# Wo multiplied into the experts' first layers and gates while edges are scattered; first layers stopped at the last node

## The chip, the core and the metric

The kernel runs on one core of one Trainium2 chip. The metric is device time in microseconds from start to end of one execution. The core's engines run side by side, each with its own instructions in a fixed order: PE (matrix multiplication, results in the PSUM memory), DVE (vectors), ACT (scalar functions and copies), POOL (here mostly for scattering by index) and SP (here a queue that starts DMA transfers). An instruction starts when its engine is free and the semaphores it waits for have been raised. Working data lie in the on-chip SBUF memory; DRAM holds inputs, outputs and scratch tensors.

## The reference

Two layers of a graph network work on 1250 nodes of 512 channels and 40000 edges. Layer 0 adds edge attention and a global linear attention to the nodes, and then a block with causal attention and a mixture of eight experts. Layer 1 has a graph convolution, an additive attention and a memory of products of keys. The change concerns the causal block and one feed-forward layer ahead of it:

```
hx = _layernorm(x, ln_g, ln_b)
q, k, v = hx @ Wq, hx @ Wk, hx @ Wv
...
attn = softmax(where(causal, q @ k.T, lowest))
o = attn @ v
y = o.transpose(0, 2, 1, 3).reshape(b, n, d) @ Wo
gate = softmax(y @ gate_W + gate_b)
hid = gelu(einsum('bnd,edf->bnef', y, W1) + b1)
eo = einsum('bnef,efd->bned', hid, W2) + b2
out = einsum('bned,bne->bnd', eo, gate)
```

So y is used in two products only, with gate_W (512 x 8) and with each expert's W1 (512 x 256). The layer ahead is `h = silu(z @ W1.T + b1); ff = h @ W2.T + b2`, with 1024 hidden channels.

## The kernel before

All data are float32, except one-hot matrices in bfloat16. The nodes are padded from 1250 to 1280 (NP) and lie in NT = 10 tiles of P = 128; the last tile has TAIL = 98 real ones. Activations that a matmul sums over lie transposed, channels on partitions, as [128, KC = 4, 1280]. Matmuls over all nodes go by three chunks of columns (CHUNKS): 512, 512 and 256. A float32 matmul stands in the profile as two records, a transpose as one.

The stages follow each other in the program:

1. **Edges.** POOL scatters 40000 edge weights into a table in DRAM (adj, 1280 x 1280 x 9 numbers) with 313 indirect DMAs (line 341). DVE compares keys (lines 315 and 325), PE counts with the one-hot matrices (line 307). `pump` lets the edges advance a few batches whenever a piece of other work has been written down, so that layer 0's linear attention and the projections of the edge attention stand among them. This stage has no order written by hand: a scheduler sets the order of instructions on each engine. Its last part is the pool gqkv (lines 521 to 575): keys and queries (kT, q_d), values (line 548), then two products of weights for layer 1. The first is gcn_Wg times dense_W, kept in DRAM as wgd_d (lines 556 to 562); then come a row of biases (bsum_d, line 568) and fold_q (lines 569 to 574, on PE as tr<-bd). Weights here share the tag "w" with three buffers, outgoing blocks the tag "qs" with three. DMAs of this part are issued on SP.
2. **Edge attention** (lines 581 to 737): for each tile a slab of adj (5760 KB) and its queries are loaded on SP (load_tile, lines 588 to 596). The first slab waits for the scatters and for everything that lay in its place in SBUF. Scores are line 617, ACT's copy of the counts is line 601, DVE's mask line 609.
3. **Feed-forward** (lines 787 to 875): the edge attention's output, then first_layer (lines 804 to 810), 8 blocks of channels by three chunks, and the second layer by tiles (line 857). On its way it loads the four weights of the causal block (fw, line 847).
4. **Causal attention** (lines 884 to 1131), with an order written by hand on PE, DVE and ACT: a loop over 40 steps (tile t, pair of heads m). A step's PE work is, in this order: transposes of one head's weights (turn, e = 0, line 1034), the preparation of a coming tile (turn_heads as ut, hx, heads, projected), turn for e = 1, divide and output for a tile that is done, the next scores (sc), and values (av, line 1047). In the step in which output stands, hx and turn_heads stand too, as long as a tile is left to prepare. ACT and DVE keep the same order: ACT does turn's copies, two exponentials (line 1023), the copies fkT and qt (line 980) and two quarters of h (line 930); DVE does the maxima (line 1007), the other two quarters of h (line 933), and the copies of turn for e = 1 (wT, line 1036), which av reads. DVE's h waits for ACT's h. output (lines 1070 to 1075) multiplies a tile's attention by Wo, 16 matmuls of 128 columns (y), and DVE copies the result into yT.
5. **Experts** (lines 1140 to 1474): gate_logits multiplies yT by gw (gate_W padded to 32 columns), hidden multiplies yT by an expert's W1 (chan_mm, in all three chunks), expert_out by its W2. load_expert fetches the next but one expert's weights on SP.
6. **Layer 1** (lines 1475 to 1841).

Nearly all plain matmuls go through `mm`, so their line is 177; their tiles' names tell them apart.

Of the kernel before, what the change touches and what calls it, by code (L numbers as in the profile page):

```python
# [11 lines left out]
F32 = mybir.dt.float32  # L12
# [55 lines left out]
def tile_gps_layers(ctx: ExitStack, tc: tile.TileContext, a, out):  # L68
# [40 lines left out]

    fold_q = const.tile([P, KC, HG], F32, name="fold_q")  # L110
    nc.gpsimd.memset(fold_q, 0.0)
    cols = const.tile([P, NCOL], F32, name="cols")
    nc.scalar.dma_start(cols, a["cols"])

# [61 lines left out]
        for i, (l, r) in enumerate(pairs):  # L176
            nc.tensor.matmul(ps, lhsT=l, rhs=r, start=i == 0, stop=i == len(pairs) - 1)  # L177

    def node_mm(ps, xT, t, w, n0=0, n1=C):

        mm(ps, [(xT[:, c, t * P:(t + 1) * P], w[:, c, n0:n1]) for c in range(xT.shape[1])])

    def chan_mm(ps, w, m, xT, c0, cn):

# [8 lines left out]
    xb_d = dram.tile([NP, C], F32, name="xb_d")  # L193
    att_d = dram.tile([P, KC, NP], F32, name="att_d")
    deg_d = dram.tile([P, NP], F32, name="deg_d")
    wgd_d = dram.tile([P, KC, C], F32, name="wgd_d")
    bsum_d = dram.tile([P, C], F32, name="bsum_d")

# [322 lines left out]
    with tc.tile_pool(name="gqkv", bufs=2) as pq:  # L521
        gbv = rows_bc(pq, a["gnn_rows"][0:2], 2, name="gbv")
        wk = load_w(pq, "gnn_WkT", KC, C, bufs=3)
        wq = load_w(pq, "gnn_WqT", KC, C, bufs=3)
        wv = load_w(pq, "gnn_WvT", KC, C, bufs=3)
        zT = pq.tile([P, KC, NP], F32, name="zT", bufs=1)
        for t in range(NT):
            z = pq.tile([P, C], F32, tag="z", name="z")
            norm(pq, z, xn[:, t, :], 1e-5, "lnz")
            transposed(zT, z, t, "att_g", "att_b")  # L530
            xb = pq.tile([P, C], F32, tag="xb", name="xb")
            nc.vector.tensor_tensor(xb, xn[:, t, :], gbv[:, 1, :], op=OP.add)
            nc.scalar.dma_start(xb_d[t * P:(t + 1) * P, :], xb)
        for c0, cn in CHUNKS:
            for m in range(KC):
                ps = ps_mm()
                chan_mm(ps[:, :cn], wk, m, zT, c0, cn)
                nc.vector.tensor_scalar(kT[:, m, c0:c0 + cn], ps[:, :cn], col("gnn_bk", m), None, op0=OP.add)
                ps = ps_mm()
                chan_mm(ps[:, :cn], wq, m, zT, c0, cn)  # L540
                qs = pq.tile([P, 512], F32, tag="qs", name="qs", bufs=3)
                nc.scalar.activation(qs[:, :cn], ps[:, :cn], AF.Identity, bias=col("gnn_bq", m))
                nc.sync.dma_start(q_d[:, m, c0:c0 + cn], qs[:, :cn])
                pump(1)
        for t in range(NT):
            ps = ps_mm()
            node_mm(ps, zT, t, wv)
            nc.vector.tensor_tensor(va[:, t, :], ps, gbv[:, 0, :], op=OP.add)
            pump(1)


        brow = rows_bc(pq, a["l1_rows"], len(L1_ROWS), name="l1rows")
        wg = load_w(pq, "gcn_WgT", KC, C, bufs=3)
        wd = load_w(pq, "L1_gnn_W_dense", KC, C, bufs=3)
        wqn = load_w(pq, "l1_Wq", KC, C, bufs=3)
        for m in range(KC):
            ps = ps_mm()
            mm(ps, [(wg[:, c, m * P:(m + 1) * P], wd[:, c, :]) for c in range(KC)])
            qs = pq.tile([P, 512], F32, tag="qs", name="qs", bufs=3)
            nc.scalar.copy(qs, ps)  # L560
            nc.sync.dma_start(wgd_d[:, m, :], qs)
            pump(1)
        ps = ps_mm()
        mm(ps, [(col("gcn_b", c).to_broadcast([P, P]), wd[:, c, :]) for c in range(KC)])
        qs = pq.tile([P, 512], F32, tag="qs", name="qs", bufs=3)
        nc.vector.tensor_tensor(qs, ps, brow[:, 0, :], op=OP.add)
        nc.vector.tensor_tensor(qs, qs, brow[:, 1, :], op=OP.add)
        nc.sync.dma_start(bsum_d, qs)
        bd = pq.tile([P, KC, H], F32, name="bd")
        nc.vector.tensor_tensor(bd, own_head, col("l1_wq", 0, 4)[:, :, None].to_broadcast([P, KC, H]), op=OP.mult)  # L570
        ps = ps_tr((P, KC, H))
        for m in range(KC):
            mm(ps[:, m, :], [(wqn[:, c, m * P:(m + 1) * P], bd[:, c, :]) for c in range(KC)])
        nc.scalar.copy(fold_q[:, :, :H], ps)
        pump(EC)
    s_edge.close()
    s_xn.close()
# [167 lines left out]

    X = ctx.enter_context(tc.tile_pool(name="X", bufs=1)).tile([P, NT, C], F32, name="X")
    s_y = ctx.enter_context(ExitStack())
    yT = s_y.enter_context(tc.tile_pool(name="fy", bufs=1)).tile([P, KC, NP], F32, name="yT")
    s_fw = s_y.enter_context(ExitStack())
    pfw = s_fw.enter_context(tc.tile_pool(name="fw", bufs=1, side="right"))  # L750

# [35 lines left out]
    with tc.tile_pool(name="gff", bufs=1) as pf, tc.tile_pool(name="gffw", bufs=2) as pw:  # L787
# [16 lines left out]
        def first_layer(c, m):  # L804
            c0, cn = CHUNKS[c]
            if m == 0:
                hTs[c] = pw.tile([P, 8, 512], F32, tag="hT", name="hT")
            ps = ps_mm()
            chan_mm(ps[:, :cn], w1, m, zT, c0, cn)
            nc.scalar.activation(hTs[c][:, m, :cn], ps[:, :cn], AF.Silu, bias=col("gnn_b1", m))  # L810
# [5 lines left out]
        with tc.manual_schedule(engines={nc.tensor.engine, nc.vector.engine, nc.scalar.engine}):  # L816
            for t in range(NT + 2):
# [26 lines left out]
                if t >= NT - 2:  # L844
                    for m in range(2 * (t - NT + 2), 2 * (t - NT + 3)):
                        first_layer(0, m)
            fw = [load_w(pfw, f"L0_ffn_W{x}", KC, C, tag="fw" + x) for x in "kqvo"]
            fetch_xm(0)
            fetch_xm(1)
            for c, (c0, cn) in enumerate(CHUNKS):  # L850
                n = cn // P
                for k, t in enumerate(range(c0 // P, c0 // P + n)):
# [1 line left out]
                        for m in range(8 * k // n, 8 * (k + 1) // n):  # L854
                            first_layer(c + 1, m)
                    ps = ps_mm()
                    node_mm(ps, hTs[c], k, w2)
                    nc.vector.tensor_tensor(X[:, t, :], ps, X[:, t, :], op=OP.add)
                    nc.vector.tensor_tensor(X[:, t, :], X[:, t, :], inputs.pop(t), op=OP.add)
                    if t + 2 < NT:  # L860
                        fetch_xm(t + 2)
# [21 lines left out]
    pmw = s_mw.enter_context(tc.tile_pool(name="moe0", bufs=2))  # L883
    with (tc.tile_pool(name="fatt", bufs=1) as pf, tc.tile_pool(name="fattw", bufs=2) as pw,
          tc.tile_pool(name="fpsum", bufs=1, space=PSUM) as psum):
        wk, wq, wv, wo = fw
        gains = pf.tile([P, 2], F32, name="gains")
        for x, name in enumerate(("kn_g", "qn_g")):
            g0 = COLS[name][0]
# [1 line left out]
                nc.sync.dma_start(gains[half(e), x:x + 1], a["cols"][:D, g0:g0 + 1])  # L891
        nc.vector.tensor_scalar_mul(gains, gains, 8.0)

        gw = pmw.tile([P, KC, HG], F32, name="gw", bufs=1)
        nc.gpsimd.memset(gw, 0.0)
        nc.sync.dma_start(gw[:, :, :NEXP], a["L0_ffn_gate_W"].rearrange("(c p) o -> p c o", p=P))
        gb = rows_bc(pmw, a["L0_ffn_gate_b"], 1, NEXP, name="gb")
        eb2 = pmw.tile([P, C], F32, name="eb2", bufs=1)
        for j in range(P // HG):
            nc.sync.dma_start(eb2[j * HG:j * HG + NEXP, :], a["L0_ffn_b2"])  # L900
        w1 = pmw.tile([P, KC, 256], F32, tag="w1", name="w1")
        nc.sync.dma_start(w1, a["L0_ffn_W1"][0].rearrange("(c p) o -> p c o", p=P))
        w2 = pmw.tile([P, 2, C], F32, tag="w2", name="w2")
        nc.sync.dma_start(w2, a["L0_ffn_W2"][0].rearrange("(c p) o -> p c o", p=P))
        experts = {0: (w1, w2)}
# [156 lines left out]
        def divide(t):  # L1062
            ps = ps_one("bc")
            for m in range(KC):
                nc.tensor.matmul(ps[:, m, :], lhsT=spread[:, m, :], rhs=tiles[t]["rd"], start=True, stop=True)
            bs = pf.tile([P, KC, P], F32, name="bs")
            nc.scalar.copy(bs, ps)
            nc.vector.tensor_tensor(tiles[t]["att"], tiles[t]["att"], bs, op=OP.mult)

        def output(t):  # L1070
            ps = ps_one("y")
            for m in range(KC):
                chan_mm(ps[:, m, :], wo, m, tiles[t]["att"], 0, P)
            del tiles[t]
            nc.vector.tensor_copy(yT[:, :, t * P:(t + 1) * P], ps)

        steps = [(t, m) for t in range(NT) for m in range(KC)]

# [11 lines left out]

        with tc.manual_schedule(engines={nc.tensor.engine, nc.vector.engine, nc.scalar.engine}):
            prep[0] = {"h": h0}
            for i in range(-6, len(steps) + 4):
                now, last, nxt = pair(i), pair(i - 1), pair(i + 1)
                due = [tile_at(i, j) for j in range(5)]
                if now:
# [21 lines left out]
                    turn(*last, 1)  # L1118
                if due[3] is not None:
                    unit_scales(due[3])  # L1120
                for k, f in ((2, divide), (3, output)):
                    x = pair(i - k)
                    if x and x[1] == KC - 1:
                        f(x[0])
                if nxt:
                    score(*nxt)
                if last:
# [24 lines left out]

    def load_expert(e):
        w1 = pmw.tile([P, KC, 256], F32, tag="w1", name="w1")
        nc.sync.dma_start(w1, a["L0_ffn_W1"][e].rearrange("(c p) o -> p c o", p=P))
        w2 = pmw.tile([P, 2, C], F32, tag="w2", name="w2")
        nc.sync.dma_start(w2, a["L0_ffn_W2"][e].rearrange("(c p) o -> p c o", p=P))
        return w1, w2
# [43 lines left out]
    def gate_logits():  # L1202

        ps = ps_big(name="lg")
        for c in range(KC):
            for g, (c0, cn) in enumerate(CHUNKS):
                nc.tensor.matmul(ps[g * HG:(g + 1) * HG, :cn], lhsT=gw[:, c, :], rhs=yT[:, c, c0:c0 + cn],
                                 start=c == 0, stop=c == KC - 1)
        for g, (c0, cn) in enumerate(CHUNKS):
            nc.scalar.copy(lgT[g * HG:(g + 1) * HG, :cn], ps[g * HG:(g + 1) * HG, :cn])  # L1210
# [30 lines left out]
                nc.vector.tensor_tensor(X[:, t, :], X[:, t, :], pss[j], op=OP.add)  # L1241

    def hidden(e, c0, cn):
        w1 = experts[e][0]
        hT = pw.tile([P, 2, 512], F32, tag="hT", name="hT")
        for m in range(2):
            ps = ps_big()
            chan_mm(ps[:, :cn], w1, m, yT, c0, cn)
            nc.scalar.activation(hT[:, m, :cn], ps[:, :cn], AF.Gelu_apprx_tanh, bias=col("moe_b1", 2 * e + m))  # L1249
        return hT  # L1250

    def expert_out(e, hT, c0, t):
        ps = ps_big()
        node_mm(ps, hT, t - c0 // P, experts[e][1])
        nc.vector.scalar_tensor_tensor(X[:, t, :], ps, gate[:, t, e:e + 1], X[:, t, :], op0=OP.mult, op1=OP.add)  # L1255

    def tiles_of(c0, cn):
        return range(c0 // P, (c0 + cn) // P)
# [652 lines left out]
```

## Time and profile before

| what | us |
|---|---|
| median of three runs (2454.78 to 2464.10) | 2463.76 |
| profiled execution | 2462.48 |
| its span, on which all stretches below stand | 2460.7 |
| PE busy | 1995.3 (81%) |
| DVE busy | 1532.5 (62%) |
| ACT busy | 771.5 (31%) |
| POOL busy | 693.9 (28%) |
| y on PE, 320 records | first at 1418.9, last from 1706.7 |

The stages start at about these times in the span: edges 0, edge attention 776 (first scores 793.85), feed-forward 1169 (first matmul 1178.07), causal attention 1374, experts 1707.76, layer 1 2016.

The table of stretches has for each stretch of time the busy microseconds and, in brackets, the number of instructions of each engine, with PE's weight loads (PEld) apart since they overlap with matmuls. PEclk is the clock granted to PE, as a share of full speed. A timeline line has the start, the duration, the engine, the line of the kernel, the operation, output and inputs, the shapes and a count; the bracket at its end is how long the engine had been idle before, and what ended that. The chain is the work that ended last, followed back. The profile takes a busy PE from modelled ends of matmuls, so a full PE can still have been waiting inside a group.

### The profile page before, as it was taken

How to read it: one execution, taken by the hardware profiler on the slowest of the kernel's cores; microseconds unless marked ns; L12 is line 12 of the kernel's file. 1: busy time of each engine (PE TensorE's matmuls, PEld its weight loads, DVE VectorE, ACT ScalarE, POOL GpSimd, SP SyncE). 2: the span in 40 equal slices, each digit the busy share in tenths (PEclk: the TensorE clock that was granted, in tenths of full speed). 3: DMA queues.
4: the chain of work that ended last, by engine and by line, in shares of the span. 5: the costliest groups of instructions: out<-in, count | busy, mean ns of one | idle time of the engine just before them, and what ended most of it. 6: DMA issues, size and time to landing. Idle time of an engine off the chain costs nothing.

```text
span 2460.7 us, 29582 instructions
## 1 busy us (share of the span) xinstructions
PE 1995.3 (81%) x10676; PEld 1183.6 (48%) x10676; DVE 1532.5 (62%) x4878; ACT 771.5 (31%) x1422; POOL 693.9 (28%) x448
## 2 busy tenths in 40 slices
PE   0396666763796899998899899999999999988852
PEld 0143344431353566666345466677445455565531
DVE  4529987799851999997513445563212232679998
ACT  0100000100001676766321466554111132245553
POOL 2017888888884000000000000000000000036555
PEclk9996777775898999999899999999899999989976
DMA  9994443455656565561700100002210010000000
GB/s 376 423 376 80 85 65 41 60 95 114 148 91 198 194 232 181 219 244 31 252 9 26 36 1 1 1 1 85 76 35 26 26 56 22 22 22 9 9 9 16
DMA packets 124526, 245.81 MB, mean 100 GB/s; under 512 B 50909, under 2 KB 79254, under 8 KB 122716
## 3 DMA queue, kind: packets, MB, share of 16 engines
q1 hardware_dynamic: 72512, 224.14, 24.4%
q0 software_dynamic: 46512, 8.02, 7.3%
q10 hardware_dynamic: 5356, 11.77, 1.3%
q8 instruction: 84, 1.38, 0.2%
q14 instruction: 62, 0.51, 0.1%
HBM read 155.81 MB, written 88.08 MB: 99 GB/s over the span
## 4 chain that ended last, share of the span: by engine, by line
PE 55%; DVE 14%; ACT 7%; DMA 2%; issue 1%; SPq 0%; ACTq 0%; DVEq 0%
PE mm L177 27%; PE one L666 4%; PE sc L617 4%; ACT wT L657 3%; PE ag L1323 3%; PE one L656 2%; PE av L1047 2%; DVE eqx L325 2%; PE sc L993 2%; PE one L1034 2%; DVE eq L315 2%; PE y L177 2%; PE conv L1440 1%; PE conv L1435 1%; DVE sc L1676 1%
## 5 line engine op out<-in xcount | busy, mean ns | idle before, releaser
L341 POOL DMA_INDIRECT adj<-tot,idx x313 | 497.0, 1588 | 262.7 <-DMA kr<-key_d 161.0
L646 DVE SCALAR_TENSOR_TENSOR ex<-ex,slab 128x1280 f32<-128x1280 f32 x80 | 197.0, 2502 | 0.0
L1255 DVE SCALAR_TENSOR_TENSOR X<-mm,gate,X 128x512 f32<-128x512 f32 x80 | 60.0, 750 | 202.4 <-PE mm L177 202.3
L325 DVE TENSOR_SCALAR_CACHE_REDUCE eqx<-kr,key 128x384 bf16<-128x384 f32 (+1 forms) x312 | 175.5, 597 | 0.0
L315 DVE SCALAR_TENSOR_TENSOR eq<-kr,key,upto 128x128 bf16<-128x128 f32 (+2 forms) x313 | 144.6, 475 | 7.8 <-PE even L307 7.6
L177 PE MATMUL mm<-w,hT 128*128 128x512 f32 x320 | 145.3, 606 | 0.0
L657 ACT COPY wT<-one 128x512 f32<-128x512 f32 (+1 forms) x240 | 116.0, 517 | 93.4 <-PE one L656 88.7
L656 PE MATMUL one<-ident,ex 128*128 128x128 f32 x800 | 125.8, 286 | 23.8 <-ACT wT L657 20.3
L177 PE MATMUL mm<-yT,w 128*128 128x512 f32 (+1 forms) x384 | 142.8, 525 | 0.8 <-issue 0.8
L627 DVE CUSTOM_DVE_ANT_0 ex<-sc,none 128x1280 f32<-128x1280 f32 x80 | 115.7, 1484 | 14.3 <-PE sc L617 13.3
L617 PE MATMUL sc<-kT,q 64*128 64x512 f32 (+1 forms) x480 | 104.5, 559 | 21.4 <-DMA q<-q_d 18.0
L656 PEld LDWEIGHTS one<-ident,ex 128*128 128x128 f32 x800 | 84.5, 141 | 66.8 <-ACT wT L657 48.3
L639 ACT ACTIVATE ex<-ex,low 128x1280 f32<-128x1280 f32 x80 | 104.8, 1361 | 10.4 <-DVE low L632 10.4
L177 PEld LDWEIGHTS mm<-yT,w 128*128 128x128 f32 x384 | 73.5, 192 | 69.1 <-issue 65.8
L666 PE MATMUL one<-wT,gva 128*64 128x128 f32 x1600 | 103.6, 288 | 3.4 <-ACT wT L657 1.8
L307 PEld LDWEIGHTS <-eq 128*128 128x128 bf16 x625 | 41.8, 105 | 130.9 <-DVE eq L315 97.7
L603 POOL DMA_DIRECT2D deg_d<-cnt x10 | 8.4, 844 | 337.8 <-ACT attT L673 315.0
L307 PEld LDWEIGHTS <-eqx 128*128 128x128 bf16 x930 | 46.8, 101 | 117.7 <-DVE eqx L325 101.9
L666 PEld LDWEIGHTS one<-wT,gva 128*64 128x64 f32 x1600 | 93.9, 145 | 13.3 <-ACT wT L657 13.3
L1036 DVE COPY wT<-one 128x512 f32<-128x512 f32 (+3 forms) x72 | 37.6, 559 | 99.0 <-PE one L1034 92.0
L177 PEld LDWEIGHTS mm<-w,hT 128*128 128x128 f32 x320 | 62.3, 195 | 76.1 <-issue 75.7
L1249 ACT ACTIVATE hT<-mm,cols 128x512 f32<-128x512 f32 (+1 forms) x48 | 29.4, 616 | 215.9 <-PE mm L177 215.9
(482 smaller groups left out, 4076.6 us busy)
## 6 DMA issues: line engine op xcount, KB each, us to landing
adj<-zrow SPq DMA_DIRECT2D x4, 14400.0 KB
slab<-adj SPq DMA_DIRECT2D x10, 5760.0 KB
kr<-key_d SPq DMA_DIRECT2D x50, 576.0 KB, 4.0
w<-in_L_ffn_W SPq DMA_DIRECT2D x16, 512.0 KB, 3.5
cnt_d<-cnt SPq DMA_DIRECT2D x10, 640.0 KB, 3.0
deg_d<-cnt POOLq DMA_DIRECT2D x10, 640.0 KB, 7.4
adjT<-cnt_d SPq DMA_DIRECT2D x5, 1280.0 KB
adj<-tot,idx POOLq DMA_INDIRECT x313, 3.3
```

Of the source, the lines that this page charges most:

```text
L177: nc.tensor.matmul(ps, lhsT=l, rhs=r, start=i == 0, stop=i == len(pairs) - 1)
L307: nc.tensor.matmul(acc[:, k, :], lhsT=eq[:, k * P:(k + 1) * P], rhs=weights, start=start and k == 0, stop=True, skip_group_check=True)
L315: nc.vector.scalar_tensor_tensor(eq[:, :n], kr[:, k0 * P:k0 * P + n], key[:, c0 + c:c0 + c + 1], upto[:, B - 1 - c:, :].rearrange("p c x - ...
L325: nc.vector.tensor_scalar(eq[:, :n * P], kr[:, k0 * P:(k0 + n) * P], key[:, c0 + c:c0 + c + 1], None, op0=OP.is_equal, op1=OP.add, accum_o ...
L341: st = nc.gpsimd.indirect_dma_start(out=adj, out_offset=bass.IndirectOffsetOnAxis(ap=idx[:, c:c + 1], axis=0), in_=tot[:, c, :], in_offset ...
L617: nc.tensor.matmul(sc[e][:, d0:d0 + dn], lhsT=q[half(e), m, :], rhs=kT[half(e), m, d0:d0 + dn], start=True, stop=True)
L627: nc.vector.tensor_tensor_reduce(out=ex, in0=sc[e][:, :NP], in1=none, scale=-0.125, scalar=-LOWEST, op0=OP.add, op1=OP.min, accum_out=low[ ...
L639: nc.scalar.activation(exs[e], exs[e], AF.Exp, bias=low[:, e:e + 1], scale=-1.0)
L646: nc.vector.scalar_tensor_tensor(exs[e], exs[e], 1.0, sl[:, :, hd], op0=OP.mult, op1=OP.mult, accum_out=den[:, hd:hd + 1])
L656: nc.tensor.transpose(ps[:, k, :], weights[t, m][e][:, (d0 + k) * P:(d0 + k + 1) * P], ident)
L657: nc.scalar.copy(wT[:, d0:d0 + dn, :], ps[:, :dn])
L666: nc.tensor.matmul(av[half(e), 0, :], lhsT=va[:, d, hd * D:(hd + 1) * D], rhs=turned[e][:, d, :], start=d == 0, stop=d == NT - 1)
```

## The change

- In the edge stage's pool gqkv, behind fold_q, a new block loads Wo of the causal block, transposes it with 16 matmuls into woT (ACT copies), multiplies Wo by gate_W into fold_g, which stays in SBUF, and Wo by the eight experts' W1, two at a time: 64 matmuls of 512 columns, 16 copies on ACT, 8 loads of 512 KB and 32 stores of 128 KB on SP. The products lie in a new DRAM tensor, w1f_d. fold_g is cleared on POOL at the start.
- In the causal attention, output goes, with its 160 matmuls and ten copies. divide writes the divided attention into aT, which takes yT's place. The loop has one step less at its end, in which nothing but the last output stood.
- The experts read W1's product from w1f_d, the gates use fold_g in place of gw, and both multiply aT.
- fw loads three weights, not four.
- first_layer and hidden compute 226 columns in the last chunk, not 256; the second layers use 98 rows of the last tile.

```diff
+        wo = load_w(pq, "L0_ffn_Wo", KC, C, bufs=3)
+        woT = pq.tile([P, KC, C], F32, tag="w", name="woT", bufs=3)
+        for k in range(KC):
+            ps = ps_tr((P, KC, P))
+            for c in range(KC):
+                nc.tensor.transpose(ps[:, c, :], wo[:, c, k * P:(k + 1) * P], ident)
+            nc.scalar.copy(woT[:, k, :].rearrange("p (c q) -> p c q", c=KC), ps)
+        gws = pq.tile([P, KC, NEXP], F32, name="gws")
+        nc.sync.dma_start(gws, a["L0_ffn_gate_W"].rearrange("(c p) o -> p c o", p=P))
+        ps = ps_tr((P, KC, NEXP))
+        for m in range(KC):
+            mm(ps[:, m, :], [(woT[:, c, m * P:(m + 1) * P], gws[:, c, :]) for c in range(KC)])
+        nc.scalar.copy(fold_g[:, :, :NEXP], ps)
+        for e in range(0, NEXP, 2):
+            w1s = pq.tile([P, 2, KC, 256], F32, tag="w", name="w1s", bufs=3)
+            for x in range(2):
+                nc.sync.dma_start(w1s[:, x], a["L0_ffn_W1"][e + x].rearrange("(c p) o -> p c o", p=P))
+            for m in range(KC):
+                ps = ps_mm((P, 2, 256))
+                mm(ps, [(woT[:, c, m * P:(m + 1) * P], w1s[:, :, c, :]) for c in range(KC)])
+                qs = pq.tile([P, 512], F32, tag="qs", name="qs", bufs=3)
+                nc.scalar.copy(qs, ps.rearrange("p x o -> p (x o)"))
+                for x in range(2):
+                    nc.sync.dma_start(w1f_d[e + x, :, m, :], qs[:, x * 256:(x + 1) * 256])
         pump(EC)
...
-            fw = [load_w(pfw, f"L0_ffn_W{x}", KC, C, tag="fw" + x) for x in "kqvo"]
+            fw = [load_w(pfw, f"L0_ffn_W{x}", KC, C, tag="fw" + x) for x in "kqv"]
...
-        nc.sync.dma_start(w1, a["L0_ffn_W1"][0].rearrange("(c p) o -> p c o", p=P))
+        nc.sync.dma_start(w1, w1f_d[0])
...
-            nc.vector.tensor_tensor(tiles[t]["att"], tiles[t]["att"], bs, op=OP.mult)
-
-        def output(t):
-            ps = ps_one("y")
-            for m in range(KC):
-                chan_mm(ps[:, m, :], wo, m, tiles[t]["att"], 0, P)
-            del tiles[t]
-            nc.vector.tensor_copy(yT[:, :, t * P:(t + 1) * P], ps)
+            nc.vector.tensor_tensor(aT[:, :, t * P:(t + 1) * P], tiles.pop(t)["att"], bs, op=OP.mult)
...
-                nc.tensor.matmul(ps[g * HG:(g + 1) * HG, :cn], lhsT=gw[:, c, :], rhs=yT[:, c, c0:c0 + cn],
+                nc.tensor.matmul(ps[g * HG:(g + 1) * HG, :cn], lhsT=fold_g[:, c, :], rhs=aT[:, c, c0:c0 + cn],
...
-        w1 = experts[e][0]
+        w1, cn = experts[e][0], columns_of(c0, cn)
...
-            chan_mm(ps[:, :cn], w1, m, yT, c0, cn)
+            chan_mm(ps[:, :cn], w1, m, aT, c0, cn)
```

Here columns_of(c0, cn) is min(cn, N - c0).

More of the change, by code (lines that the diff above doesn't have):

```diff
@@ L111, in tile_gps_layers @@
     nc.gpsimd.memset(fold_q, 0.0)
+    fold_g = const.tile([P, KC, HG], F32, name="fold_g")
+    nc.gpsimd.memset(fold_g, 0.0)
     cols = const.tile([P, NCOL], F32, name="cols")
@@ L177, in mm, with node_mm, nodes_of, columns_of @@
             nc.tensor.matmul(ps, lhsT=l, rhs=r, start=i == 0, stop=i == len(pairs) - 1)
-    def node_mm(ps, xT, t, w, n0=0, n1=C):
-        mm(ps, [(xT[:, c, t * P:(t + 1) * P], w[:, c, n0:n1]) for c in range(xT.shape[1])])
+    def node_mm(ps, xT, t, w, rows=P):
+        mm(ps[:rows], [(xT[:, c, t * P:t * P + rows], w[:, c, :]) for c in range(xT.shape[1])])
+    def nodes_of(t):
+        return TAIL if t == NT - 1 else P
+    def columns_of(c0, cn):
+        return min(cn, N - c0)
     def chan_mm(ps, w, m, xT, c0, cn):
@@ L195, in tile_gps_layers @@
     deg_d = dram.tile([P, NP], F32, name="deg_d")
+    w1f_d = dram.tile([NEXP, P, KC, 256], F32, name="w1f_d")
     wgd_d = dram.tile([P, KC, C], F32, name="wgd_d")
@@ L747, in tile_gps_layers @@
     s_y = ctx.enter_context(ExitStack())
-    yT = s_y.enter_context(tc.tile_pool(name="fy", bufs=1)).tile([P, KC, NP], F32, name="yT")
+    aT = s_y.enter_context(tc.tile_pool(name="fy", bufs=1)).tile([P, KC, NP], F32, name="faT")
     s_fw = s_y.enter_context(ExitStack())
@@ L807, in first_layer @@
                 hTs[c] = pw.tile([P, 8, 512], F32, tag="hT", name="hT")
+            cn = columns_of(c0, cn)
             ps = ps_mm()
@@ L856, in tile_gps_layers @@
                     ps = ps_mm()
-                    node_mm(ps, hTs[c], k, w2)
-                    nc.vector.tensor_tensor(X[:, t, :], ps, X[:, t, :], op=OP.add)
+                    r = nodes_of(t)
+                    node_mm(ps, hTs[c], k, w2, r)
+                    nc.vector.tensor_tensor(X[:r, t, :], ps[:r], X[:r, t, :], op=OP.add)
                     nc.vector.tensor_tensor(X[:, t, :], X[:, t, :], inputs.pop(t), op=OP.add)
@@ L885, in tile_gps_layers @@
           tc.tile_pool(name="fpsum", bufs=1, space=PSUM) as psum):
-        wk, wq, wv, wo = fw
+        wk, wq, wv = fw
         gains = pf.tile([P, 2], F32, name="gains")
@@ L892, in tile_gps_layers @@
         nc.vector.tensor_scalar_mul(gains, gains, 8.0)
-        gw = pmw.tile([P, KC, HG], F32, name="gw", bufs=1)
-        nc.gpsimd.memset(gw, 0.0)
-        nc.sync.dma_start(gw[:, :, :NEXP], a["L0_ffn_gate_W"].rearrange("(c p) o -> p c o", p=P))
         gb = rows_bc(pmw, a["L0_ffn_gate_b"], 1, NEXP, name="gb")
@@ L1092, in tile_gps_layers @@
             prep[0] = {"h": h0}
-            for i in range(-6, len(steps) + 4):
+            for i in range(-6, len(steps) + 3):
                 now, last, nxt = pair(i), pair(i - 1), pair(i + 1)
@@ L1120, in tile_gps_layers @@
                     unit_scales(due[3])
[L1121 to L1124, printed above, removed]
+                x = pair(i - 2)
+                if x and x[1] == KC - 1:
+                    divide(x[0])
                 if nxt:
@@ L1154, in load_expert @@
         w1 = pmw.tile([P, KC, 256], F32, tag="w1", name="w1")
-        nc.sync.dma_start(w1, a["L0_ffn_W1"][e].rearrange("(c p) o -> p c o", p=P))
+        nc.sync.dma_start(w1, w1f_d[e])
         w2 = pmw.tile([P, 2, C], F32, tag="w2", name="w2")
@@ L1252, in expert_out @@
     def expert_out(e, hT, c0, t):
-        ps = ps_big()
-        node_mm(ps, hT, t - c0 // P, experts[e][1])
-        nc.vector.scalar_tensor_tensor(X[:, t, :], ps, gate[:, t, e:e + 1], X[:, t, :], op0=OP.mult, op1=OP.add)
+        ps, r = ps_big(), nodes_of(t)
+        node_mm(ps, hT, t - c0 // P, experts[e][1], r)
+        nc.vector.scalar_tensor_tensor(X[:r, t, :], ps[:r], gate[:r, t, e:e + 1], X[:r, t, :], op0=OP.mult,
+                                       op1=OP.add)
     def tiles_of(c0, cn):
```

## The prediction

> **What bounds the kernel now.** I read the table of stretches first (one line per 50 us; after the width come the busy times of PE, PE's weight loads, DVE, ACT and POOL, then PE's granted clock, the DMA share and GB/s), because the change takes work from one stage and puts it into another.
>
> ```profile
> 550.00:600.00 50.00, 19.50 (x147) 9.99 (x147) 49.94 (x211) 0.81 (x4) 42.08 (x27) 0.59 0.52 102
> 700.00:750.00 50.00, 49.83 (x179) 28.35 (x177) 15.57 (x58) 2.58 (x5) 40.93 (x27) 1.00 0.42 62
> 1550.00:1600.00 50.00, 50.00 (x351) 32.92 (x351) 25.57 (x75) 30.89 (x60) 0.00 (x0) 1.00 0.00 1
> 1800.00:1850.00 50.00, 50.00 (x126) 23.66 (x125) 11.01 (x15) 5.44 (x9) 0.00 (x0) 1.00 0.09 32
> ```
>
> Under the edge scatter PE has 30 us of 50 free at 550 us, when DVE is full and POOL issues its scatters, but none at 700 us. In the causal attention (1375 to 1707) and the experts (1707 to 2015) PE is full. So it matters where under the scatter the new work stands. Next I read PE's, POOL's and the chain's lines around the scatter's end.
>
> ```profile
> 720.67 34.50 PE L177 MATMUL mm<-gnn_WvT,zT 128*128 128x512 f32 x80
> 755.01 13.90 PE L177 MATMUL mm<-L_gnn_W_dense,gcn_WgT 128*128 128x512 f32 x32
> 771.67 1.55 POOL L341 DMA_INDIRECT adj<-tot,idx  x1 [0.30 <-issue]
> 772.17 3.63 PE L177 MATMUL tr<-bd,l_Wq 128*128 128x8 f32 x32
> 773.88 2.01 DMA bsum_d<-qs
> 776.52 17.20 DMA q<-q_d
> 793.85 4.50 PE L617 MATMUL sc<-kT,q 64*128 64x512 f32 x12 [18.04 <-DMA q<-q_d]
> ```
>
> POOL's last scatter and PE's last weight product end within 3 us of each other. The first slab is issued on SP at 776.15, once bsum_d has landed, and scores start 17.70 us after that issue. Anything that PE adds before the slab's issue is late by its whole length. Last, one attention step in which y is made (tile 6's output, during tile 7):
>
> ```profile
> 1611.82 0.80 ACT L930 ACTIVATE h<-hx,cols 128x128 f32<-128x128 f32 x2
> 1612.65 0.73 DVE L933 TENSOR_SCALAR h<-hx,cols 128x128 f32<-128x128 f32 x2 [5.33 <-ACT h L930]
> 1613.30 1.28 DVE L1036 COPY wT<-one 128x512 f32<-128x512 f32 x2
> 1608.43 3.74 PE L177 MATMUL y<-attT,L_ffn_Wo 128*128 128x128 f32 x32
> 1612.10 1.99 PE L993 MATMUL sc<-fkT,qt 64*128 64x512 f32 x8
> 1614.02 1.98 PE L1047 MATMUL av<-wT,fva 128*64 128x128 f32 x32
> ```
>
> While PE runs y, DVE stands 5.33 us behind ACT's h, which is queued behind ACT's table load, two exponentials and two copies. Only then come DVE's h and the wT copy that av needs: its first half ends at about 1613.9, and av starts at 1614.02. PE looks full, yet y fills a wait that is there anyway.
>
> **The edge stage: the added work.** The built order of the changed kernel keeps PE's order up to tr<-bd and puts all 96 new matmuls behind it, directly ahead of the scores; SP's first slab stands behind all 32 new w1f_d stores. The sum, from PE's end at 775.80:
> - 16 transposes in four groups with two PSUM buffers: four cost 0.43 to 0.60 (tr<-ident,z), an ACT copy of 128x512 0.59; with three waits for copies 3.1 us, 778.9.
> - 16 gate matmuls of 8 columns, 32 records as in the 772.17 line: 3.6, of which 0.2 overlap: 782.3.
> - 64 matmuls of 128x512, two records each at 34.50/80 = 0.431: 55.2, 837.5. The operand is read in two runs of 256 columns, for which no row exists; as two 256-column records (1.73 for eight) it would be 55.4, so both ends agree.
> - The last copy 0.7 (838.2), two store issues (838.6), landing 2.0 (bsum_d) to 2.8 (the median of a 128 KB q_d store), 0.26 of SP's waits: slab at 840.9 to 841.7, taken 841.3. That is 65.2 behind 776.15, and scores follow it by the same 17.7.
> - Clock: the small matmuls and waits may let it sink; nothing to 3.4 us, taken 0.8. Together **+66**, bounds 63 and 71.
>
> Hidden: Wo's load waits for wg's slot (768.9), 1 MB lands in 5.4 to 5.6 (L_mix_Wq, Wo), about 774.5, 1.3 us ahead of need. The first w1s pair stands behind bsum_d's store and the release of a slot at 773 to 776; two loads of 512 KB at 3.5 each end by 781.5, needed at 782.3; without that cover the 2 us in the upper bound. Later pairs have 13.8 us of matmuls each, and stores of 2.8 us a block of 3.45. Behind SP's stores nothing waits but the slab; ACT's and DVE's next work (cnt, none) waits for the slab too. The gate_W load moved ahead of some key loads is one issue of 0.3 us on SP, which POOL's even pace of 27 scatters in 50 us hides. fold_g's memset stands ahead of zrow's on POOL: 0.16 (padded, 0.49 for three), taken as **+0.2**.
>
> **The attention: y removed.** Ten y of 3.57 on PE, and the copies of 0.68 on DVE. If all PE time were path: 9 x 3.57, and for the last one 1707.76 - 1701.49 = 6.3, in all 38.4. But av can move forward only to its wT copy. That gives 0.4 for y(0) (copy ends 1422.70, av at 1423.18), nothing for y(1), y(2) and y(4), and 0.1 to 0.2 for y(3), y(5), y(6): 0.8 in all. y(7) and y(8) have no h to wait for, as no tile is left to prepare: 7.1. With the last one 14.2. The first pass of the loop shows what a step without y does, because it has none:
>
> ```profile
> 1396.10 0.43 PE L1047 MATMUL av<-wT,fva 128*64 128x128 f32 x2
> 1398.50 0.43 PE L1047 MATMUL av<-wT,fva 128*64 128x128 f32 x2 [1.96 <-DVE wT L1036]
> 1399.13 5.14 PE L177 MATMUL mm<-L_ffn_Wk,h 128*128 128x512 f32 x8
> ```
>
> The wait stands open, and the matmuls behind it take 4.94 instead of 3.44, the clock being 0.50 in 1400 to 1402. The other short gaps here cost the same way: behind 2.08 us at 1372 the eight take 5.90 (and the ones ahead of them 0.9 more), behind 1.5 us at 1700 y takes 5.44 instead of 3.57. The seven new gaps are 3.1 to 3.5 long. At 1.5 to 3.3 a gap (I take 1.7, nearest the two plain rows), seven of them and the one that y(9) paid and the first expert matmuls now pay: 8 x 1.7 = 13.6. **Attention: -14.2 + 13.6 = -0.6**; bounds -38.4 and +12 (8 x 3.3 - 14.2).
>
> The Trainium skill's page "TensorE: Matmul & The Clock Gate", Part 1: The HAM clock gate, says that the clock halves after an idle window of about 3.4 us that runs free. By it gaps of 3.1 to 3.5 us would seldom fill a window, the 13.6 would mostly fall away and the total would be about 2510. The rows above lost the clock after 1.5 to 2 us, so I go by them.
>
> **The last 30 columns.** Eight 256-column records take 1.73, so 0.0253 less each at 226. 64 records in the first GNN layers and 128 in the experts, both stages with PE full: **-4.9**; bounds 0 and -4.9, and I take the full one since 512 to 256 scales exactly. The 98-row stationaries still stream 512 columns: nothing.
>
> **Sum.** The profiled execution took 2462.48 (span 2460.7), 1.3 below the median of 2463.76, within the spread of the three runs. 2462.5 + 66 + 0.2 - 0.6 - 4.9 = **2523**, slower by 2.4%.
>
> **Rivals.**
> - Gaps without clock loss: 2523 - 13.6 = 2510. For it: 2.9 us idle at 1726 were followed by full clock until 1730. Against: the three rows above. Chance 0.18.
> - DVE's wT copy is no bound, and all of y is saved: 2462.5 + 66.2 - 4.9 - 38.4 = 2485. For it: PE is listed full. Against: av starts within 0.2 us of the copy's first half behind y(1), y(3), y(4), y(5) and y(6). Chance 0.11.
> - The other side: the products run in PE's free time under the scatter. Then the 66 go, and even with the attention's -0.6 the time is 2457; with all of y saved 2419. It decides if the W1 products are done by 776, that is begun by 714. For it: 30 us of 50 are free at 550. Against: the order is fixed, and PE is full from 650 on. Chance 0.02.
> - Loads or a sunk clock stretch the products: at 71 for the edges and +12 for the attention 2541. Chance 0.07.
>
> The page "Perfetto Trace Analysis", Optimization Strategy, advises to interleave regimes with different busiest engines, which this change does; by that rule the third rival's 2419 would be the time. The stretch at 700 us shows the regime's last part is PE's own.
>
> The forecast itself has 0.62. Its own range is 2515 to 2532. The range goes down to 2484, which takes in the first two rivals, and up to 2537, the edge's upper bound with most of the attention's; the third rival, half of the last and thin tails, about 0.15, are left out. A measurement tells 0.5% (12 us) from no change here: faster has 0.02, within 0.5% 0.02, slower 0.96.
>
> **What would show it.** Right: PE busy without gap from 776 to about 838, the slab issued near 841 and scores near 859; seven gaps over 3 us ahead of av, ended by DVE's wT, with a clock of 0.5 behind each; attention from ut to the first expert matmul within 6 us of its 333. Wrong: W1 products before 714; the slab issued ahead of the last store; av without gaps.

## The result: slower by 2.5%, and the profile after

The changed kernel takes 2519.63 us (median of four runs, 2516.46 to 2526.93) against 2459.41 for the kernel before, timed beside it: a ratio of 1.0252, with a 95% interval of 1.0231 to 1.0272. The profiled execution took 2519.92, its span is 2518.1, 57.4 longer than before's 2460.7. PE's busy time went from 1995.3 to 2029.6: the new products outweigh what y and the trims took off.

The new products stand where the prediction put them. PE's timeline around the end of the scatter in the changed kernel (start, duration, records, idle before) is:

```profile
770.30 3.78 PE L180 MATMUL tr<-bd,l_Wq 128*128 128x8 f32 x32
773.94 3.50 PE L591 MATMUL tr<-ident,L_ffn_Wo 128*128 128x128 f32 x16
777.50 4.33 PE L180 MATMUL tr<-gws,woT 128*128 128x8 f32 x32
781.68 57.96 PE L180 MATMUL mm<-w1s,woT 128*128 128x512 f32 x128
861.11 4.64 PE L652 MATMUL sc<-kT,q 64*128 64x512 f32 x12 [21.46 <-DMA q<-q_d]
```

PE works without a break from tr<-bd to 839.6. Then it stands for 21.46 us until the queries and the slab are there. The chain of waits of the same execution has what lies between the last product and the scores:

```profile
781.83 57.83 PE mm L180 x128
...
839.72 0.59 ACT qs L607
840.33 0.32 SPq L609
...
840.70 1.81 DMA w1f_d<-qs
842.65 0.32 SPq L626
...
843.02 17.20 DMA q<-q_d
860.23 0.88 issue
861.11 4.66 PE sc L652 x12
```

Last copy, its store, the store's landing, then the slab at 842.65 (before: 776.15): each link is one that the prediction added up. The scores come 67.3 us later than before (861.11 - 793.85).

In the causal attention the gaps ahead of av stand open. These are PE's lines; the first is the gap that before had too, the others lie where y(0) to y(6) had stood:

```profile
1462.62 0.43 PE L1081 MATMUL av<-wT,fva 128*64 128x128 f32 x2 [1.96 <-DVE wT L1070]
1486.91 1.04 PE L1081 MATMUL av<-wT,fva 128*64 128x128 f32 x6 [2.71 <-DVE wT L1070]
1513.87 1.14 PE L1081 MATMUL av<-wT,fva 128*64 128x128 f32 x10 [3.25 <-DVE wT L1070]
1543.56 1.09 PE L1081 MATMUL av<-wT,fva 128*64 128x128 f32 x14 [3.54 <-DVE wT L1070]
1575.89 2.40 PE L1081 MATMUL av<-wT,fva 128*64 128x128 f32 x18 [1.62 <-DVE wT L1070]
1610.55 2.82 PE L1081 MATMUL av<-wT,fva 128*64 128x128 f32 x22 [1.57 <-DVE wT L1070]
1647.44 3.25 PE L1081 MATMUL av<-wT,fva 128*64 128x128 f32 x26 [1.36 <-DVE wT L1070]
1687.13 1.96 PE L1081 MATMUL av<-wT,fva 128*64 128x128 f32 x30 [1.15 <-DVE wT L1070]
```

The last four look short because the wait is split there. These are the engines' lines in the last of them (the heads of tile 8 are turned, and y(6) is missing), to be held against the six lines that the prediction shows of before:

```profile
1684.92 0.80 ACT L964 ACTIVATE h<-hx,cols 128x128 f32<-128x128 f32 x2
1685.75 0.73 DVE L967 TENSOR_SCALAR h<-hx,cols 128x128 f32<-128x128 f32 x2 [5.32 <-ACT h L964]
1686.40 1.28 DVE L1070 COPY wT<-one 128x512 f32<-128x512 f32 x2
1681.63 1.98 PE L1027 MATMUL sc<-fkT,qt 64*128 64x512 f32 x6
1684.50 1.12 PE L1027 MATMUL sc<-fkT,qt 64*128 64x512 f32 x2 [0.89 <-ACT fkT L1014]
1685.55 0.43 PE L1081 MATMUL av<-wT,fva 128*64 128x128 f32 x2
1687.13 1.96 PE L1081 MATMUL av<-wT,fva 128*64 128x128 f32 x30 [1.15 <-DVE wT L1070]
```

The scores start earlier by y's length, then wait 0.89 for ACT's fkT, then av waits 1.15 for DVE's wT. From hx's start (1607.12 before, 1680.22 after) to av's long run it is 6.90 us in before and 6.91 here: nothing of y's 3.57 us on PE was saved. And the clock sinks behind a gap (the table of stretches; PEclk is the third number from the end):

```profile
1514.00:1516.00 2.00, 2.00 (x14) 1.65 (x15) 0.77 (x4) 0.38 (x2) 0.00 (x0) 0.58 0.00 0
1516.00:1518.00 2.00, 2.00 (x4) 0.70 (x3) 0.00 (x0) 1.56 (x5) 0.00 (x0) 0.56 0.02 4
1518.00:1520.00 2.00, 2.00 (x6) 0.88 (x5) 0.00 (x0) 0.00 (x0) 0.00 (x0) 1.00 0.00 0
```

Where the 57.4 us lie, read from the starts of the same instructions in both traces:

| stretch | before | after | difference |
|---|---|---|---|
| start to first scores | 793.85 | 861.11 | +67.3 |
| scores to first matmul of the first GNN layer | 423.78 | 422.28 | -1.5 |
| first GNN layer to ut (trim) | 156.79 | 155.15 | -1.6 |
| ut to first expert matmul (y gone) | 333.34 | 328.09 | -5.3 |
| first expert matmul to the last group of 16 (trim) | 299.16 | 297.57 | -1.6 |
| last group of expert matmuls to the end | 453.78 | 453.90 | +0.1 |

The change touches neither the second row nor the last. Without any edit in it the stretch of the second row took 418.1 to 425.3 us in the twelve profiles of this document, so its -1.5 says nothing.

### The profile page after: what moved, and what is told of

Read it like the earlier page. It is cut to its first block, busy times and chain, and to the rows that moved or that the text cites. A ratio compares the mean times of both kernels' runs of the same rounds, so it can differ in the third digit from the quotient of the medians.

```text
span 2518.1 us, 29393 instructions
## 1 busy us (share of the span) xinstructions
PE 2029.6 (81%) x10532; PEld 1184.0 (47%) x10532; DVE 1526.9 (61%) x4868; ACT 781.9 (31%) x1443; POOL 696.2 (28%) x448
## 3 DMA queue, kind: packets, MB, share of 16 engines
q8 instruction: 83, 1.36, 0.2%
## 4 chain that ended last, share of the span: by engine, by line
PE 55%; DVE 14%; ACT 9%; DMA 2%; issue 1%; SPq 0%; ACTq 0%; DVEq 0%
PE mm L180 29%; PE one L701 4%; PE sc L652 4%; ACT wT L692 3%; PE ag L1350 3%; PE av L1081 2%; PE one L691 2%; DVE eqx L335 2%; PE one L1068 2%; PE sc L1027 2%; DVE eq L325 2%; PE conv L1467 1%; PE conv L1462 1%; DVE sc L1703 1%; PE simps L1628 1%
## 5 line engine op out<-in xcount | busy, mean ns | idle before, releaser
L180 PE MATMUL mm<-w,hT 128*128 128x512 f32 (+1 forms) x320 | 145.7, 608 | 0.0
L180 PE MATMUL mm<-faT,w 128*128 128x512 f32 (+1 forms) x384 | 140.3, 519 | 0.7 <-ACT bs L1101 0.7
L180 PEld LDWEIGHTS mm<-faT,w 128*128 128x128 f32 x384 | 73.5, 192 | 67.0 <-issue 66.0
L180 PEld LDWEIGHTS mm<-w,hT 128*128 128x128 f32 (+1 forms) x320 | 61.7, 194 | 76.5 <-issue 76.4
```

## The experiments

Ten kernels ran. Their before was timed beside them and had medians of 2458.65 to 2460.82. The ratios and their intervals are not quotients of the two medians and can differ a little from them. Differences between two kernels in the same stage are taken from the profiles.

### The parts alone

**Without the products.** The block behind tr<-bd is gone; the experts read W1 and the gates gate_W as they stand, so the multiplication by Wo is left out.

```diff
-        wo = load_w(pq, "L0_ffn_Wo", KC, C, bufs=3)
...
-                    nc.sync.dma_start(w1f_d[e + x, :, m, :], qs[:, x * 256:(x + 1) * 256])
+        nc.sync.dma_start(fold_g[:, :, :NEXP], a["L0_ffn_gate_W"].rearrange("(c p) o -> p c o", p=P))
...
-        nc.sync.dma_start(w1, w1f_d[e])
+        nc.sync.dma_start(w1, a["L0_ffn_W1"][e].rearrange("(c p) o -> p c o", p=P))
```

> Leaves out the multiplication of W1 and of the gates by Wo: the experts read W1 and the gates gate_W as they stand; the rest is the changed kernel. Theory (the parts add up): the scores, which were 67.3 us later than before, stand where they stood, and the fold_g memset stays: 2519.6 - 67.3 = about 2452 (2450 to 2455), so 5 to 9 us faster than before; the attention from ut to the first expert product stays at 328. Rival (the later stages only look shorter because the edge stage disturbs them, or take back part of the 67): 2459 or more, no gain over before.

Measured: 2453.57 (ten runs), ratio 0.9984 (0.9966 to 1.0002); scores at 795.82. The median lies 7.3 below that of before, the ratio stands for 3.9, and its interval also allows nothing. The attention took 331.20 where 328 was expected, with the same gaps.

**The products alone,** in the kernel before:

```diff
         nc.scalar.copy(fold_q[:, :, :H], ps)
+        wo = load_w(pq, "L0_ffn_Wo", KC, C, bufs=3)
...
+                    nc.sync.dma_start(w1f_d[e + x, :, m, :], qs[:, x * 256:(x + 1) * 256])
```

> The kernel before with the products of Wo alone added under the edge stage, written out and read by nobody; y is still computed and nothing is trimmed. Theory (nothing hides the products): scores at 861, 67 later, and all of it stays to the end: 2459.4 + 67.3 = about 2527 (2524 to 2531). Rival (half of the 60 us came from the removed y and the trims being worth nothing): 2520 or less; and if later stages take part of it back, 2490 to 2515.

Measured: 2526.43, ratio 1.0275 (1.0237 to 1.0313), scores at 861.78. The products cost 66 us by the medians and nothing later takes it back. The loss of the whole change is theirs.

**The trims alone,** in the kernel before:

```diff
+    def columns_of(c0, cn):
+        return min(cn, N - c0)
...
+            cn = columns_of(c0, cn)
             ps = ps_mm()
             chan_mm(ps[:, :cn], w1, m, zT, c0, cn)
...
-        w1 = experts[e][0]
+        w1, cn = experts[e][0], columns_of(c0, cn)
```

> The kernel before, with the last 30 node columns left out of the first GNN layers and the experts' first layers, and 98 rows in their second layers for the last tile. Theory (both stages have PE full, 192 records at 0.0253 us): 4.9 less, a record of 226 columns at 0.190 to 0.192, the time 0.998 of before. Rival (another engine ends these stages, or the clock eats it): no difference.

Measured: 2449.37 (twelve runs), ratio 0.9961 (0.9948 to 0.9974): 9.6 less, 6.4 to 12.8 by the interval, more than the 4.9. The instruction groups of PE in this kernel (records, busy us, mean ns) give the size in the two stages:

```profile
L177 PE MATMUL mm<-yT,w 128*128 128x226 f32 x128 | 27.0, 365 | 0.0
L177 PE MATMUL mm<-zT,gnn_W1T 128*128 128x226 f32 x64 | 12.9, 354 | 0.0
```

Before, the same groups had 30.2 and 14.5. The first GNN layers' stage is 1.59 shorter and the experts' 2.65, together 4.2. The other 4.3 us by which this profile's span is shorter (2452.2 against 2460.7) lie in stages that the edit does not touch. The end from the last group of expert matmuls alone, which no experiment edits, took between 448.2 and 457.6 us in the eleven profiles besides before's. Why the median of twelve runs lies lower than the two stages explain stays open.

### The gap and its clock

**A filler.** Where y(1) to y(6) stood, PE gets 16 matmuls of the same shape that nobody reads.

```diff
+        def filler(t):
+            ps = ps_one("y")
+            for m in range(KC):
+                chan_mm(ps[:, m, :], wv, m, aT, t * P, P)
...
+                x = pair(i - 3)
+                if x and x[1] == KC - 1 and 1 <= x[0] <= 6:
+                    filler(x[0])
```

> The changed kernel with 16 matmuls of 128x128 put back on PE where y(1) to y(6) stood, their result read by nobody: more work and nothing else. Theory (the six steps lose time through the clock that sinks in the gap, the gap itself is covered): 2519.6 - 9.0 = about 2511 (2508 to 2513), the six gaps closed and the clock full behind them. Rival (the clock has no part, the steps are longer through DVE or ACT): 2519 to 2520. Rival (PE's work counts in full): 2519.6 + 6 x 3.57 = 2541.

Measured: 2510.24, ratio 1.0202 (1.0173 to 1.0231): 9.4 us faster than the changed kernel by the medians, with 192 records more. PE's timeline of the step that had the gap of 3.25, and the clock behind it:

```profile
1513.99 3.74 PE L180 MATMUL y<-faT,L_ffn_Wv 128*128 128x128 f32 x32
1517.66 0.92 PE L1027 MATMUL sc<-fkT,qt 64*128 64x384 f32 x4
1518.50 0.97 PE L1081 MATMUL av<-wT,fva 128*64 128x128 f32 x12
```

```profile
1518.00:1520.00 2.00, 2.00 (x20) 1.31 (x17) 1.60 (x6) 0.27 (x2) 0.00 (x0) 1.00 0.00 0
1520.00:1522.00 2.00, 2.00 (x6) 0.82 (x5) 0.00 (x0) 1.67 (x5) 0.00 (x0) 1.00 0.02 4
```

PE does 3.74 us of useless work, av starts no later for it, and the clock stays at 1.00. The attention goes from 328.09 to 317.60. Of the 10.5 us, 2.7 lie in the steps of the first tile, which the edit leaves alone and which ran at a higher clock in this profile; 7.8 lie in the steps of y(1) to y(5). So the gaps did cost clock, and y's PE time was free in these steps.

**The exponentials later.** In the steps that turn a new tile's heads, ACT runs fkT, qt and h first.

```diff
-                if now:
+                late = due[0] is not None or due[4] is not None
+                if now and not late:
                     exponentials(*now)
...
                     hx(due[0])
+                if now and late:
+                    exponentials(*now)
```

> The changed kernel, and in each attention step that turns the heads of a new tile ACT runs fkT, qt and h ahead of the two exponentials, not behind them. Theory (av waits for DVE's wT copy, which is queued behind h, which waits for ACT): h and wT come about 3.5 us earlier, the seven gaps and their clock loss go, and each y removed is really saved: 6 x 3.57 for y(1) to y(6), 9.0 of clock, 3.6 for y(0), 3.7 for the gap that before had too: about 37 less than 2519.6, 2483 (2478 to 2490). Rival (the exponentials, 2.9 us later, hold the transposes of the next step): 2500 to 2520. Rival (the waits are PSUM buffers that exponentials do not release): 2519.

Measured: 2490.00, ratio 1.0117 (1.0087 to 1.0147), the upper end of the expected range. The attention is 295.48, 32.6 shorter than in the changed kernel; the gaps for wT that are left are 0.45 to 1.25 us. The steps of y(0) to y(6) are now 2.0 to 3.6 us shorter than in the kernel before, where y took 3.57. The chain wT behind h behind ACT's queue is what held y's gain.

**The same move in the kernel before.**

> The kernel before, with the same move of the exponentials behind fkT, qt and h. Theory (there y covers the wait for wT, so that only the one open gap of 1.96 us with its 1.7 us of clock goes): 2460.8 - 4 = about 2457, attention from ut to the first expert product 326 to 331. Rival (the move is worth its 30 us by itself, y or not): about 2431.

Measured: 2457.42, ratio 0.9995 (0.9979 to 1.0012); attention 333.20 against 333.34. The rival is out. Of the small gain expected, 4 us, the runs show none clear of their spread: the one open gap shrank from 1.96 to 1.25 and still cost 1.7 us of clock, the tiles up to the ninth became 1.4 us shorter in sum, and the last one 1.2 longer. An order worth 30 us without y is worth next to nothing with it.

### What the first slab waits for

**The stores on ACT's queue:**

```diff
-                    nc.sync.dma_start(w1f_d[e + x, :, m, :], qs[:, x * 256:(x + 1) * 256])
+                    nc.scalar.dma_start(w1f_d[e + x, :, m, :], qs[:, x * 256:(x + 1) * 256])
```

> The changed kernel with the 32 stores of w1f_d issued by ACT, so that SP's queue holds no store ahead of the first slab. Theory of the prediction (the slab stands behind the stores in SP's queue): the slab goes out once the w1s loads are through, by about 815, its 17 us run under the products, and scores follow PE's end at 840: 861 - 21, the time 2519.6 - 21 = about 2498. Rival (the slab's place in SBUF is that of tiles which the stores still read, whoever issues them): slab again near 842, 2516 to 2523.

Measured: 2520.07, ratio 1.0264 (1.0231 to 1.0298). SP's queue is clear after the loads, and the slab goes out no earlier (timeline of SP, then SP's waits between 760 and 870 us: total, times, longest):

```profile
775.04 38.09 SPq L602 DMA_DIRECT2D w1s<-in_L_ffn_W  x8
842.64 0.34 SPq L626 DMA_DIRECT2D slab<-adj  x1
```

```profile
SPq L626 <- DMA w1f_d<-qs: 29.0, 7, 19.0
```

The slab stands in SP's queue in seven waits, 29 us in all, for stores that another engine issues.

**The slab's pool on the other side of SBUF,** besides:

```diff
-          tc.tile_pool(name="gattw", bufs=2) as pw,
+          tc.tile_pool(name="gattw", bufs=2, side="right") as pw,
```

> As stores_act, and the pool of the slab laid on the other side of SBUF, over the edges' tiles, which are free once the last scatter is in. Theory (queue and place together): slab by about 815, scores right behind PE's last product at 840, about 2498 (2494 to 2503); so 21 of the 67 us are the slab's load behind the products, 46 the products' own. Rival (neither holds the slab, something else does): slab near 842, 2516 to 2523.

Measured: 2523.34, ratio 1.0260 (1.0226 to 1.0294); the slab goes out at 848.81, behind products that ended at 845.8, and the scores start at 867.05. So it is not SP's order, and moving the pool did not free it. Whether part of the slab still lies where the products' tiles lay, or the slab waits for all DMAs ahead of it, was not separated.

### A place for the products

**Early.** The same products, cut into 21 pieces (4 for the transposes, 1 for the gates, 16 of four matmuls), stand in the last loop of layer 0's linear attention, with W1 in the place of a tile that is dead by then.

```diff
+    def products(pm, pfold):
+        wo = load_w(pm, "L0_ffn_Wo", KC, C, bufs=2)
...
+        w1s = pm.tile([P, 2, 2, KC, 256], F32, tag="a", name="w1s")
...
             x_t = load_x(t)
+            if t == 0:
+                fold = products(pm, pfold)
+            next(fold, None)
             ps = ps_mm()
             node_mm(ps, hid, t, w2)
+            if t:
+                next(fold, None)
...
+            if t > 6:
+                next(fold, None)
             pump(1)
```

> The changed kernel with the same products cut into 21 pieces and issued between the last loop of the mix stage, at 500 to 600 us, where PE is busy for half of the time, and not behind tr<-bd; all else as in the changed kernel. Theory (POOL's scatters pace this stretch, PE and ACT have the room, DVE gets no work): scores at 794 again, 67 less than the changed kernel, 2453 (2448 to 2460). Rival (PE's pieces of 3.5 us hold up the edges' matmuls, DVE at 99% has no slack and the scatters fall behind): 2465 to 2500.

Measured: 2452.67, ratio 0.9974 (0.9958 to 0.9991), 67 less than the changed kernel. The table of stretches shows the room filled and POOL's pace unchanged. The first line is of the kernel before, whose next stretch, with 19.50, is the prediction's first line; the two others are of this kernel:

```profile
500.00:550.00 50.00, 30.78 (x172) 13.79 (x170) 50.00 (x212) 1.01 (x5) 41.94 (x27) 0.66 0.53 104
500.00:550.00 50.00, 45.86 (x249) 23.73 (x248) 46.04 (x193) 6.11 (x15) 40.37 (x26) 0.90 0.80 197
550.00:600.00 50.00, 47.77 (x232) 21.00 (x231) 50.00 (x212) 6.78 (x15) 42.07 (x27) 1.00 0.74 165
```

The last scatter is issued at 771.88 (before 771.67). PE's own tail comes 5 us later, with the wgd products at 759.97 instead of 755.01, and the scores at 798.98. What delays the tail is not shown: the products ended at 602.6, and in 600 to 650 PE was busy for 22.68 us only.

**Combined.** Early, the exponentials later, and in the same steps the second head's transposes and wT copy ahead of ut and hx:

```diff
+                if last and late:
+                    turn(*last, 1)
                 if due[4] is not None:
                     turn_heads(due[4])
...
-                if last:
+                if last and not late:
                     turn(*last, 1)
```

> The kernel of early, with the exponentials moved as in exps_late and the transposes and DVE copy of the second wT put ahead of ut and hx in the same steps, so that the copy no longer stands behind h. Theory: the products cost nothing (2453), the move gives the 30 us measured, and the 4 us of waits for wT that are left there go: 2453 - 34 = about 2419 (2414 to 2428), faster than both kernels. Rival (an earlier end of one stage opens a wait in the next): 2430 to 2450.

Measured: 2424.86, ratio 0.9858 (0.9837 to 0.9880): 1.4% faster than before, 95 us faster than the changed kernel. The attention is 296.40, no shorter than with the exponentials alone. PE's line in the step that makes the transposes of the following weights says why:

```profile
1446.07 0.55 PE L1088 MATMUL one<-ident,ex 128*128 128x128 f32 x3 [1.55 <-ACT ex L1077]
```

The wait for wT is gone and a wait for the exponentials has taken its place: seven of them, of 2.19 down to 0.24 us. That is what the rival of that run had named, a new wait behind the old one. The time lies in the range of the theory even so, but the 4 us that the second move was to bring did not come.

## Why the prediction was right, step by step

The forecast was 2523, the measured median 2519.63. The sign, the stage that loses and the gaps in the attention were as foreseen. That the sum fits so closely is in part luck, since terms that were off by some us cancel.

- **Edge stage, +66:** +67.3 in the traces, +66 by the medians of the products alone. Part of the fit is luck: PE ended tr<-bd at 774.08 in this profile and not at 775.80, which took 1.7 off, and the scores came 18.46 behind the slab's issue and not 17.70. The transposes and gates came out at 7.7 us from the end of tr<-bd to the first product (predicted 6.5), the products at 57.83 (55.2): the clock was 0.50 from 782 to 786, behind the gates' small matmuls. The clock term, taken as 0.8 and at most 3.4, is mis-sized: the products took 2.6 more than forecast and what stands ahead of them 1.2 more, 3.8 together. Copy, store and landing were 3.0 (predicted 3.8). The loads were hidden, as said.
- **"SP's first slab stands behind all 32 new w1f_d stores":** the number holds, but the order in SP's queue is not what sets it. With the stores on another queue the slab waits for their landing all the same.
- **Attention, y saved for 14.2:** y(7) and y(8) gave 3.57 each and the end 7.09, together the 14.2. The steps of y(0) to y(5) did not get shorter but longer, by 1.2 to 1.7 each and 8.9 in all; the step of y(6) stayed as it was.
- **Clock in the attention, 8 x 1.7 = 13.6:** the size per gap was right on average, the count in this profile was six before the experts: the gap of y(6) cost nothing, and the first expert matmuls pay theirs outside this stretch (8.83 against 7.10). In the four other kernels with this attention the steps of y(0) to y(6) are 11.4 to 11.7 us longer than in before, close to seven times 1.7.
- **Attention, -0.6:** without the experts' 1.7 the forecast for this stretch is -2.3. The stretch is 5.3 shorter in this pair, and 3.1 shorter on average, over the five profiles with this attention (327.86 to 331.20) and the three with the one of before (330.00 to 333.34). The first two tiles have no y in either kernel, and their steps took 39.4 to 42.8 us. Without them the average is 2.6 shorter (287.5 against 290.1). The times of whole runs do not show this gain: the trims alone took 9.6 off the median, the trims with y removed (no products) 7.3.
- **"Seven gaps over 3 us":** only two were. One was 2.71, and four were two waits one behind the other, for fkT and for wT. The delay was as foreseen, its picture was not.
- **Trim, -4.9:** 4.2 in the two stages of trims alone.
- **The rivals.** Gaps without clock loss (2510): the filler refutes it, since closing the gaps won 9.4 us. The idle time at 1726 that was named for it in fact speaks against it: the clock was 0.98 from 1728 to 1730, as read, but 0.50 from 1730 to 1734. All of y saved (2485): refuted by 6.90 against 6.91 us from hx to av; it needs another order on ACT, and then the run gave 2490. Products under the scatter (2457): not what the change does, but what the early products do, 2452.67. Loads or a sunk clock (2541): the clock did sink ahead of and in the products, by the 3.8 us above, and no load held them up.

The Trainium skill, "TensorE: Matmul & The Clock Gate", Part 1: The HAM clock gate, asks for an idle window of about 3.4 us before the clock halves. Here gaps of 2.71 to 3.54 were each followed by half clock in all five profiles that have them, and so were many of 1.0 to 1.6. What fits the page, which has full clock return after a busy window of about the same 3.4 us, is the length of the penalty: a loss of 1.7 us is 3.4 us at half clock, and the loss per step was mostly 0 or 1.7.

The Trainium skill, "Perfetto Trace Analysis", Optimization Strategy, whose advice to interleave regimes was weighed against the change, is borne out by the early products: the same work cost 67 us at the end of the regime and nothing measurable in the middle of it (2452.67 with it, 2453.57 without the products).

## What to carry to other kernels

Work "under" a bound engine was free here only where the engine that does it idled at that place in its order: look at the table of stretches slice by slice, and put the pieces there. Before removing work from an engine that looks full, find what the next instruction waits for besides it; if that comes at the same moment, the removal opens a gap, and the gap costs clock on top. Move the thing that was covered first, then remove the cover.

## What the runs showed of the hardware

The same gap does not always cost the same. The two waits of 1.00 and 1.36 us in the step that had y(5) were followed by 1.7 us of lost clock in the changed kernel, and by none in the four other kernels with this attention. In those four the step that had y(6), with waits of 0.89 and 1.15, was 1.6 longer than in before, where in the changed kernel it was not, and the steps of y(2) and y(3) were longer by 2.4 to 3.0, where in the changed kernel they were by 1.5 to 1.7. The gates' 32 records of 8 columns took 4.33 us in three profiles and 6.99 in three others of the same code, with the clock sunk though PE listed no idle time; the scores start anywhere from 860.9 to 867.1 with it. A single profile of this kernel tells such stages apart only to some us.
